# Row-tiled cluster products two at a time on the banks of the attention sums, and two filler pieces moved into the first group norm

## The chip, the cores and the metric

The kernel runs on one core of a Trainium2 chip. The metric is device time in microseconds (us), 3557.26 as the median of three runs. A core has TensorE (matrix products, written to the eight banks of PSUM), VectorE, ScalarE and GpSimd (elementwise work; GpSimd does not touch PSUM in this kernel), and queues that move data.

## What is computed

Four images of 256 channels and 64 × 64 pixels go through two layers, all in f32. Layer 0 is self-attention over the 4096 pixels with a residual:

```
attn = softmax(q k)            # 4096 x 4096 per image
x    = gamma * (v attn) + x
```

Layer 1 begins with a group norm over the whole image (`gn1`), then clusters the pixels, and adds the result to x:

```
out = sim * agg                # each pixel gets its cluster's mean, for each head
y   = x + ls1 * (proj_w out + proj_b)
```

A second group norm (`gn2`) over y, a two-layer perceptron with gelu, another residual, and a final 1 × 1 convolution with relu follow. The group norms need sums over a whole image before their first output can be had.

## The kernel before

The order of the instructions on every engine is written out by hand; each engine works its own list in that order, and an instruction waits until what it reads is there and what it overwrites is free. The main loop runs over the four images (`b`, called batches here). For each one `weighting` does the attention's sums, `cluster` the first norm and the clustering, and `mlp` the rest, including scores of the next image.

**Fillers.** While an image is in the stages with little TensorE work, TensorE is fed pieces of the next image's projections. `projections` (line 592) is a list of 35 pieces: 32 calls of `v_half` (line 271: two matmuls, and after every second call a copy by ScalarE, line 286), with `k_half(0)`, `q_four(0)` and `k_half(1)` put in ahead of number 26. `fill(n)` takes the next n pieces. Before the change they went: 8 in `weighting`, 2 in `gn1`, 10 in `cluster` ahead of the products, 4 and 9 among the products (lines 916 and 922), 2 in `gn2`. The last image has no next one, so its `fill` does nothing.

**The first norm** (`group_norm`, line 203): VectorE aggregates the statistics, TensorE averages them over the partitions (`gnm_gn`, lines 209 and 210; `gnv_gn`, line 219), `rsqrt` (line 151) goes through ScalarE and VectorE with the pooling between, and VectorE forms scale and shift. `cluster` then scales the pooled values (line 626), and TensorE makes `pcen` from them (line 631), `len` and `wc` (lines 670 to 675), and the large `fv` (line 762).

**The products.** `products(hb, c)` (line 867) adds the projected clusters to the pixels: `hb` is a half of the rows, `c` a half of the channels, and q = 0 to 3 are four matmuls of 32 rows by 512 columns, each in its own 32 rows of the array and its own PSUM bank, so that four can run at once. For c = 0 the banks are those of `ps_s` (two tiles of two banks), and VectorE adds directly (line 898). For c = 1 they were `a0` and `a1` of `ps_a`, in which the weighting sums, and both banks of `ps_m`; ScalarE scales each into a tile `cl` (line 908; three of them rotate), and GpSimd adds it (line 909). `seen` (line 863) takes the statistics of the second norm on VectorE. Those feed `bn_aggr` (line 207) and `gnm_gn` of `gn2`.

**Who else uses the banks.** `v_half`, `k_half` and `q_four` write banks of `ps_m`, which rotate in the order of allocation. `gnm_gn` and `gnv_gn` use `a0` and `a1`.

Of the kernel before, what the change touches and what calls it, by code (L numbers as in the profile page):

```python
# [8 lines left out]
F32 = mybir.dt.float32  # L9
AF = mybir.ActivationFunctionType  # L10
ALU = mybir.AluOpType
AX = mybir.AxisListType

P = 128
# [3 lines left out]
NB = 512  # L18
# [27 lines left out]
def attention_then_cluster_block(  # L46
# [17 lines left out]
    nc = tc.nc  # L64
# [9 lines left out]
    ps_a = ctx.enter_context(tc.tile_pool(name="ps_a", bufs=1, space=PSUM))  # L74
    ps_m = ctx.enter_context(tc.tile_pool(name="ps_m", bufs=2, space=PSUM))
# [67 lines left out]
    def par(name, k=None):  # L143
        i = PC.index(name)
        return pc_s[:, :, i] if k is None else pc_s[:, k, i : i + 1]
# [5 lines left out]
    def rsqrt(dst, src, eps, meanwhile=lambda: None):  # L151

        nc.vector.tensor_scalar(dst, src, eps, None, ALU.add)
        nc.scalar.activation(dst, dst, AF.Sqrt)
        meanwhile()
        nc.vector.reciprocal(dst, dst)
# [42 lines left out]
    def table(f):  # L199

        nc.scalar.activation(probe, probe, f)

    def group_norm(b, which, stats, fill, meanwhile=lambda: None):

        nm = f"{which}_{b}"
        mv = small.tile([P, 2], F32, tag="mv", name=f"mv_{nm}")
        nc.vector.bn_aggr(mv, stats.rearrange("p i s -> p (i s)"))
        ps1 = ps_a.tile([P, NB], F32, tag="a0", name=f"gnm_{nm}")
        nc.tensor.matmul(ps1[:, 0:1], left, mv[:, 0:1], start=True, stop=True)
        nc.tensor.matmul(ps1[:, 1:2], avg, mv[:, 0:1], start=True, stop=True)  # L210
        fill(1)
        dv = small.tile([P, 2], F32, tag="dv", name=f"dv_{nm}")
        nc.vector.tensor_copy(dv, ps1[:, 0:2])
        nc.vector.scalar_tensor_tensor(
            mv[:, 1:2], dv[:, 0:1], dv[:, 0:1], mv[:, 1:2], ALU.mult, ALU.add
        )
        nc.vector.tensor_scalar(dv[:, 1:2], dv[:, 1:2], -1.0, None, ALU.mult)
        ps2 = ps_a.tile([P, NB], F32, tag="a1", name=f"gnv_{nm}")
        nc.tensor.matmul(ps2[:, 0:1], avg, mv[:, 1:2], start=True, stop=True)
        rstd = small.tile([P, 1], F32, tag="rstd", name=f"rstd_{nm}")  # L220
        rsqrt(rstd, ps2[:, 0:1], GN_EPS, meanwhile)
        fill(1)
        if which == "gn2":
            table(AF.Gelu_apprx_tanh)
        ga = small.tile([P, KC], F32, tag="ga", name=f"ga_{nm}")
        gb = small.tile([P, KC], F32, tag="gb", name=f"gb_{nm}")
        nc.vector.tensor_scalar(ga, par(f"{which}_w"), rstd, None, ALU.mult)
        nc.vector.scalar_tensor_tensor(gb, ga, dv[:, 1:2], par(f"{which}_b"), ALU.mult, ALU.add)
        return ga, gb
# [369 lines left out]
    def cluster(b, ys, stats, cells, rest, fill):  # L599

        pool = small.tile([P, KC, 4, 4], F32, tag="pool", bufs=1, name=f"pool_{b}")

        def pooling():
# [3 lines left out]
            nc.vector.tensor_scalar(pool, pool, 1.0 / 256, None, ALU.mult)  # L607

        ga, gb = group_norm(b, "gn1", stats, fill, pooling)
        xns = {}  # L610

# [138 lines left out]
        for nb in range(NBLK):  # L750
# [18 lines left out]
            for g in range(2):  # L769
                q = 2 * fh + g  # L770
# [89 lines left out]
        stats2 = small.tile([P, 2 * NBLK, 6], F32, tag="stats", name=f"st2_{b}")  # L860
        pieces = {}

        def seen(hb, c):
            for q in range(4):
                nc.vector.bn_stats(stats2[:, 4 * q + 2 * hb + c, :], pieces[hb, c][q])

        def products(hb, c):
            if c == 0:
                two = [
                    ps_s.tile([P, 2, NB], F32, tag="s", name=f"op_{b}_{hb}_{c}_{f}")  # L870
                    for f in range(2)
                ]
                ops = [two[q // 2][:, q % 2, :] for q in range(4)]
            else:
                ops = [
                    pool.tile([P, NB], F32, tag=tag, name=f"op_{b}_{hb}_{c}_{q}")
                    for q, (pool, tag) in enumerate(
                        ((ps_a, "a0"), (ps_a, "a1"), (ps_m, "m"), (ps_m, "m"))
                    )
                ]  # L880
            for q in range(4):
                rows = slice(q * 32, (q + 1) * 32)
                nc.tensor.matmul(  # L883
                    ops[q],
                    g_s[rows, c * P : (c + 1) * P],
                    sim_t[rows, hb, :],
                    start=True,
                    stop=True,
                )
            pieces[hb, c] = yqs = [  # L890
                ys[2 * (q // 2) + hb][:, c, :].rearrange("p (h f w) -> p f h w", h=16, f=2)[
                    :, q % 2
                ]
                for q in range(4)
            ]
            for q in range(4):
                if c == 0:
                    nc.vector.scalar_tensor_tensor(  # L898
                        yqs[q],
                        ops[q].rearrange("p (h w) -> p h w", h=16),  # L900
                        par("ls1", c),
                        yqs[q],
                        ALU.mult,
                        ALU.add,
                    )
                else:
                    add = work.tile([P, NB], F32, tag="w", bufs=3, name=f"cl_{b}_{hb}_{q}")
                    nc.scalar.activation(add, ops[q], AF.Identity, scale=par("ls1", c))  # L908
                    nc.gpsimd.tensor_tensor(
                        yqs[q], add.rearrange("p (h w) -> p h w", h=16), yqs[q], ALU.add  # L910
                    )

        products(0, 0)
        products(0, 1)
        seen(0, 0)
        fill(4)
        products(1, 0)
        products(1, 1)
        seen(0, 1)
        seen(1, 0)  # L920
        seen(1, 1)
        fill(9)
        return stats2


    def mlp(b, ys, stats2, fill, nxt):

        ga, gb = group_norm(b, "gn2", stats2, fill)
        fill(N)
        ob = out[b].rearrange("(k p) h w -> p k (h w)", p=P)  # L930
# [97 lines left out]
    def filler(todo):  # L1028
        def fill(n):
            for _ in range(min(n, len(todo))):  # L1030
                todo.pop(0)()

        return fill

    with tc.manual_schedule():
        here = attention(0, xs0)
        here.alone()
        for b in range(B):
            xs1 = []
            nxt = attention(b + 1, xs1) if b + 1 < B else None  # L1040

            def ahead():
                if nxt and len(xs1) < N // XT:
                    xs1.append(load_x(b + 1, len(xs1)))

            fill = filler(list(nxt.projections) if nxt else [])
            stats, cells, rest = here.weighting(ahead, fill, (lambda: None) if b else derived)
            stats2 = cluster(b, here.xs, stats, cells, rest, fill)
            mlp(b, here.xs, stats2, fill, nxt)
            here = nxt  # L1050
# [76 lines left out]
```

## Time and profile before

| What | Value |
|---|---|
| median of 3 runs | 3557.26 us (3555.52 to 3558.32) |
| profiled span | 3554.6 us |
| mean granted TensorE clock | 0.990 |
| attention sums `av` (line 389) on the chain that ended last | 50% |
| products `op` (line 883), 64 matmuls | 128 records, 587 ns each |
| `cl` (line 908), 32 times | 687 ns each |

The page gives the share of the span in which each engine was busy, and the chain of work that ended last, followed back from the end. The list of waits says which instruction waited for which, in total, how often, and the longest time. The timeline has one row for neighbouring instructions of one line: start, length, engine, line, what is written and read, the number of records, and in brackets the idle time of the engine ahead and what ended it. PE is TensorE's matmul, PEld its weight load, DVE VectorE, ACT ScalarE, POOL GpSimd. PEclk is the share of its full clock that TensorE was granted.

### The profile page before, as it was taken

The page shows a single profiled execution, that of the slowest core. Times are in us where ns is not written, and L with a number is a line of the kernel's source. Part 1 is how long each engine was busy: PE and PEld are TensorE (multiplying, and loading weights), DVE is VectorE, ACT ScalarE, POOL GpSimd, SP SyncE. Part 2 cuts the span into 40 slices and gives each one's busy share as a digit, 9 for nine tenths or more (in the row PEclk, how much of TensorE's full clock was granted, in tenths as well). Part 3 has the DMA queues.
Part 4 walks back from the last instruction along what each step waited for, and adds up shares of the span by engine and source line. Part 5 has one row for each costly group of instructions (what it writes and reads, how often), then busy time and mean ns, then how long its engine had stood idle before and what let it go on. Part 6 is the DMA issues. An engine that isn't in the chain of part 4 may idle for free.

```text
span 3554.6 us, 28614 instructions
## 1 busy us (share of the span) xinstructions
PE 3467.7 (98%) x11016; PEld 1570.0 (44%) x11016; DVE 1699.8 (48%) x1972; ACT 1560.3 (44%) x1765; POOL 1380.2 (39%) x660
## 2 busy tenths in 40 slices
PE   8999999999999999999999999999999999997899
PEld 4344445644444444654444444464444444445444
DVE  3666664411366666441146666743115666664100
ACT  4555552433454554343354554533335554542222
POOL 1565665100265665410035665631004666672000
PEclk9999999999999999999999999999999999998999
DMA  2000001000000000000000000100000000000000
GB/s 89 7 4 3 6 1 48 7 18 18 12 6 4 3 6 20 29 13 12 18 15 4 3 6 3 47 1 13 18 18 9 4 6 3 4 0 1 12 18 18
DMA packets 25368, 46.93 MB, mean 13 GB/s; under 512 B 6704, under 2 KB 8592, under 8 KB 25232
## 3 DMA queue, kind: packets, MB, share of 16 engines
q1 hardware_dynamic: 20240, 38.29, 3.2%
q10 hardware_dynamic: 4992, 6.82, 0.8%
q8 instruction: 86, 1.41, 0.2%
q14 instruction: 50, 0.41, 0.0%
HBM read 19.93 MB, written 16.78 MB: 10 GB/s over the span
## 4 chain that ended last, share of the span: by engine, by line
PE 94%; DVE 3%; ACT 1%; issue 0%; DMA 0%; SPq 0%; ACTq 0%
PE av L389 50%; PE h L991 13%; PE mo L980 12%; PE sc L326 8%; PE pw L951 3%; PE vp L278 2%; PE fv L762 2%; PE mb L364 1%; PE den L410 1%; PE qp L297 0%; PE kp L255 0%; PE tt L350 0%; DVE vf L771 0%; PE op L883 0%; DVE x L898 0%
## 5 line engine op out<-in xcount | busy, mean ns | idle before, releaser
L389 PE MATMUL av<-s,v 128*128 128x512 f32 x4096 | 1826.5, 597 | 1.3 <-ACT s L379 1.3
L384 POOL TENSOR_TENSOR acc<-acc,s 128x1024 f32<-128x1024 f32 x448 | 1058.3, 2362 | 470.3 <-ACT s L379 450.7
L389 PEld LDWEIGHTS av<-s,v 128*128 128x128 f32 x4096 | 758.9, 190 | 1025.3 <-issue 1015.8
L379 ACT ACTIVATE s<-s 128x1024 f32<-128x1024 f32 x512 | 539.0, 1057 | 464.6 <-DVE s L376 431.4
L336 DVE TENSOR_TENSOR top<-sc,top 128x1024 f32<-128x1024 f32 x224 | 274.2, 1224 | 714.5 <-PE sc L326 714.5
L376 DVE TENSOR_TENSOR s<-s,mb 128x1024 f32<-128x1024 f32 x512 | 595.0, 1206 | 8.6 <-PE mb L364 8.3
L381 POOL TENSOR_TENSOR acc<-s 128x1024 f32<-128x1024 f32 x32 | 75.2, 2349 | 1133.9 <-ACT s L379 1133.9
L991 PE MATMUL h<-xn,w_s 128*128 128x512 f32 x1024 | 480.9, 597 | 4.6 <-DVE xn L937 4.6
L980 PE MATMUL mo<-hs,w_s 128*128 128x512 f32 x1024 | 476.0, 592 | 0.0
L332 ACT COPY s<-sc 128x1024 f32<-128x1024 f32 x256 | 258.5, 1010 | 406.4 <-PE sc L326 406.4
L999 ACT ACTIVATE hs<-h,pv_s 128x512 f32<-128x512 f32 x256 | 176.1, 688 | 478.6 <-PE h L991 478.6
L991 PEld LDWEIGHTS h<-xn,w_s 128*128 128x128 f32 x1024 | 192.8, 191 | 255.4 <-issue 249.6
L980 PEld LDWEIGHTS mo<-hs,w_s 128*128 128x128 f32 x1024 | 194.6, 190 | 244.9 <-issue 239.2
L337 ACT COPY s<-sc 128x1024 f32<-128x1024 f32 x256 | 259.3, 1013 | 91.6 <-DVE top L336 50.3
L339 DVE TENSOR_TENSOR top<-sc,top 128x1024 f32<-128x1024 f32 x224 | 274.4, 1225 | 49.7 <-ACT s L332 30.0
L326 PE MATMUL sc<-q,k 32*128 32x512 f32 x2048 | 295.1, 640 | 2.7 <-ACT s L337 2.7
L1018 DVE SCALAR_TENSOR_TENSOR x<-mo,pc_s,x 128x512 f32<-128x512 f32 x64 | 48.1, 751 | 495.9 <-PE mo L980 492.5
L326 PEld LDWEIGHTS sc<-q,k 32*128 32x128 f32 x2048 | 81.9, 182 | 194.8 <-issue 109.1
L278 PE MATMUL vp<-wv_s,x 128*128 128x256 f32 x512 | 132.4, 407 | 21.1 <-ACT cl L908 11.7
L278 PEld LDWEIGHTS vp<-wv_s,x 128*128 128x128 f32 x512 | 98.0, 200 | 49.6 <-ACT cl L908 16.6
L951 PE MATMUL pw<-xn,wpw_s 128*128 128x512 f32 x256 | 115.5, 594 | 0.8 <-ACT xn L1021 0.8
L334 DVE TENSOR_TENSOR top<-sc,s 128x1024 f32<-128x1024 f32 x32 | 39.2, 1225 | 146.4 <-ACT s L332 146.4
(166 smaller groups left out, 1652.6 us busy)
## 6 DMA issues: line engine op xcount, KB each, us to landing
x<-in_x SPq DMA_DIRECT2D x32, 512.0 KB, 4.7
out<-xn SPq DMA_DIRECT2D x64, 256.0 KB, 2.1
q<-q ACTq DMA_DIRECT2D x104, 64.0 KB, 2.0
w_s<-in_w SPq DMA_DIRECT2D x2, 1024.0 KB, 7.6
q<-q SPq DMA_DIRECT2D x24, 64.0 KB, 2.0
wv_s<-in_wv SPq DMA_DIRECT2D x1, 256.0 KB, 6.9
wpw_s<-in_wpw SPq DMA_DIRECT2D x1, 256.0 KB, 9.5
wfv_l<-in_wfv SPq DMA_DIRECT2D x1, 192.0 KB, 3.0
```

What stands on the lines that cost most here:

```text
L278: nc.tensor.matmul(vps[0][:, i % 2, :], xs[i * P // XT][:, k, o : o + P], wv_s[:, k, :], start=(k == 0), stop=(k == KC - 1),)
L326: nc.tensor.matmul(halves[r // 2][:, r % 2, :], k_s[rows, g, :], q_s[rows, :], start=True, stop=True)
L332: nc.scalar.copy(s[:, 0:2, :], halves[0])
L336: nc.vector.tensor_tensor(top, halves[1], top, ALU.max)
L337: nc.scalar.copy(s[:, 2:4, :], halves[1])
L339: nc.vector.tensor_tensor(top, halves[0], top, ALU.max)
L376: nc.vector.tensor_tensor(sh, sh, mxs[nb].unsqueeze(1).to_broadcast([P, 2, NB]), ALU.subtract)
L379: nc.scalar.activation(sh, sh, AF.Exp)
L384: nc.gpsimd.tensor_tensor(acc, acc, s[:, 2 * h : 2 * h + 2], ALU.add)
L389: nc.tensor.matmul(av[c], own["v"][:, RG * g + quarter, c * P : (c + 1) * P], slots[u][:, quarter, :], start=(g == 0 and quarter == 0), st ...
L980: nc.tensor.matmul(acc[c], w2_s[:, j, c * P : (c + 1) * P], hs[j], start=(j == 0), stop=(j == HID // P - 1),)
L991: nc.tensor.matmul(ps, w1_s[:, k, j * P : (j + 1) * P], xn[:, 0, k, :], start=(k == 0), stop=(k == KC - 1),)
```

## The change

The second channel half of the products (c = 1) now goes two at a time, q = 0 and 1 and then q = 2 and 3, both on `a0` and `a1`; `ps_m` is left to the fillers. Between the two pairs stand two filler pieces. The fillers are spread anew: two more in the first norm (where `fill(1)` becomes `fill(3)`), then 2, 2, 2 and 5 among the products. That is for keeping TensorE supplied while ScalarE empties the banks. In the third of these places the pieces are `k_half(0)` and `q_four(0)`. Which numbers are computed does not change.

```diff
-        fill(1)
+        fill(3 if which == "gn1" else 1)
...
-        def products(hb, c):
+        def products(hb, c, qs):
...
-                ops = [two[q // 2][:, q % 2, :] for q in range(4)]
+                ops = {q: two[q // 2][:, q % 2, :] for q in qs}
             else:
-                ops = [
-                    pool.tile([P, NB], F32, tag=tag, name=f"op_{b}_{hb}_{c}_{q}")
-                    for q, (pool, tag) in enumerate(
-                        ((ps_a, "a0"), (ps_a, "a1"), (ps_m, "m"), (ps_m, "m"))
-                    )
-                ]
-            for q in range(4):
+                ops = {
+                    q: ps_a.tile([P, NB], F32, tag=f"a{q % 2}", name=f"op_{b}_{hb}_{c}_{q}")
+                    for q in qs
+                }
+            for q in qs:
...
-        products(0, 0)
-        products(0, 1)
+        products(0, 0, range(4))
+        products(0, 1, (0, 1))
         seen(0, 0)
-        fill(4)
-        products(1, 0)
-        products(1, 1)
+        fill(2)
+        products(0, 1, (2, 3))
+        fill(2)
+        products(1, 0, range(4))
+        products(1, 1, (0, 1))
+        fill(2)
+        products(1, 1, (2, 3))
         seen(0, 1)
         seen(1, 0)
         seen(1, 1)
-        fill(9)
+        fill(5)
```

More of the change, by code (lines that the diff above doesn't have):

```diff
@@ L864, in seen @@
             for q in range(4):
-                nc.vector.bn_stats(stats2[:, 4 * q + 2 * hb + c, :], pieces[hb, c][q])
-        def products(hb, c):
+                nc.vector.bn_stats(stats2[:, 4 * q + 2 * hb + c, :], pieces[hb, c, q])
+        def products(hb, c, qs):
             if c == 0:
@@ L889, in products @@
                 )
[L890 to L896, printed above, removed]
+            for q in qs:
+                y = pieces[hb, c, q] = ys[2 * (q // 2) + hb][:, c, :].rearrange(
+                    "p (h f w) -> p f h w", h=16, f=2
+                )[:, q % 2]
                 if c == 0:
                     nc.vector.scalar_tensor_tensor(
-                        yqs[q],
+                        y,
                         ops[q].rearrange("p (h w) -> p h w", h=16),
                         par("ls1", c),
-                        yqs[q],
+                        y,
                         ALU.mult,
@@ L909, in products @@
                     nc.gpsimd.tensor_tensor(
-                        yqs[q], add.rearrange("p (h w) -> p h w", h=16), yqs[q], ALU.add
+                        y, add.rearrange("p (h w) -> p h w", h=16), y, ALU.add
                     )
-        products(0, 0)
-        products(0, 1)
+        products(0, 0, range(4))
+        products(0, 1, (0, 1))
         seen(0, 0)
-        fill(4)
-        products(1, 0)
-        products(1, 1)
+        fill(2)
[5 more added lines that the diff above has]
+        products(1, 1, (2, 3))
         seen(0, 1)
```

## The prediction

> **What bounds the kernel now.** I read the page first, its engine line and its chain that ended last:
>
> ```profile
> PE 3467.7 (98%) x11016; PEld 1570.0 (44%) x11016; DVE 1699.8 (48%) x1972; ACT 1560.3 (44%) x1765; POOL 1380.2 (39%) x660
> ...
> PE 94%; DVE 3%; ACT 1%; issue 0%; DMA 0%; SPq 0%; ACTq 0%
> ```
>
> TensorE is the bound nearly everywhere. So a change pays where it takes TensorE's idle time away, or where it raises the granted clock. Next, the list of TensorE's waits (total us, times, longest); two of its lines lie in the edited stages:
>
> ```profile
> PE gnm_gn L209 <- DVE mv_gn L207: 17.0, 5, 10.8
> PE vp L278 <- ACT cl L908: 11.7, 6, 2.0
> ...
> PE pcen L631 <- DVE pool L626: 8.4, 4, 2.8
> ```
>
> The second line is six waits of a filler (`v_half`) on the scaling copy `cl`, two in each of batches 0 to 2: the filler wants a bank of `ps_m` that products 2 and 3 of the second half still occupy. The third is the gap in the first norm, ahead of the pooled centres. Batch 0's timeline shows both in place (columns: start, length, instruction, and in brackets the idle time ahead):
>
> ```profile
> 613.20 1.11 PE L278 MATMUL vp<-wv_s,x 128*128 128x256 f32 x4
> 616.17 0.48 PE L631 MATMUL pcen<-pool,mix 128*96 128x16 f32 x4 [1.85 <-DVE pool L626]
> ...
> 621.25 5.07 PE L762 MATMUL fv<-mix,xn 128*128 128x208 f32 x20
> ```
>
> ```profile
> 661.81 2.00 PE L883 MATMUL op<-simt,g 32*128 32x512 f32 x16
> 665.72 3.72 PE L278 MATMUL vp<-wv_s,x 128*128 128x256 f32 x16 [1.91 <-ACT cl L908]
> 669.37 2.00 PE L883 MATMUL op<-simt,g 32*128 32x512 f32 x16
> 673.35 1.99 PE L278 MATMUL vp<-wv_s,x 128*128 128x256 f32 x8 [1.98 <-ACT cl L908]
> ```
>
> Each f32 matmul leaves two records here, so a `v_half` is four records and two sets of four products are sixteen. The bracketed waits show 3.89 us of idle TensorE per batch around the products, and 1.85 us in the norm. Last, the busy time and granted clock of successive windows behind that norm (columns: window; length; busy time of PE, PEld, DVE, ACT, POOL with instruction counts; PEclk; DMA):
>
> ```profile
> 613.83:617.24 3.41, 1.56 (x11) 1.10 (x9) 2.73 (x11) 1.40 (x2) 0.00 (x0) 1.00 0.00 0
> 617.24:620.65 3.41, 3.41 (x13) 2.80 (x12) 2.46 (x9) 0.96 (x2) 0.00 (x0) 0.50 0.02 5
> 620.65:624.06 3.41, 3.41 (x11) 3.15 (x11) 0.00 (x0) 0.59 (x1) 0.00 (x0) 0.50 0.00 0
> 624.06:627.47 3.41, 3.41 (x21) 3.41 (x20) 1.22 (x4) 1.52 (x2) 0.56 (x1) 1.00 0.00 0
> ```
>
> After a stretch with only 1.56 us of work in 3.41, TensorE runs at half clock for 6.8 us. The same happens from 1487.6 (busy 1.55) and from 2361.4 (busy 1.55). Around the products only one gap did it: 1542.25 to 1545.67 was busy for 1.45 us, and 3.41 us at half clock followed. Windows there with 1.92 us of work or more stayed at full clock.
>
> [...] sixteen records in 2.00 us is two sets of four, some 0.86 us a set once the 0.15 us tail is taken off. [...] The trace's cost is small: from 665.72 to 669.37 is 3.65 us for 16 filler records, which at their pace elsewhere (24 in 5.25 us, 0.219 each) need 3.50, hence 0.15 going in; coming back out of a tiled mode (678.74 to 680.58) takes 0.12 more than the preceding 1.72 us step.
>
> **The change, part by part.**
>
> Two fillers into the first norm: two `v_half`, 2 × 4 × 0.219 = 1.75 us. The run of three begins at 613.20 and ends about 615.9; `pcen` started at 616.17, because VectorE's pooled values came at 616.03. So they lie inside the wait, at no cost, and 1.75 us of filler leave the product stage. ScalarE gets one copy more (0.59 us) there, which pushes the first norm's activation from 615.73 to about 616.6; its output is not needed before `fv` starts, so nothing is paid.
>
> The clock behind it: with the gap filled, the window has over 3 us of work, and the clock should stay. At full clock `vp` behind `pcen` ends near 617.4, `len` starts at 617.6 (VectorE's operand is ready at 617.55), the `wc` group ends about 618.8, the next `vp` 0.88 us later, and `fv` starts at 619.8 in place of 621.25. That is 1.45 us; the cold 2.8 us of `fv` up to 624.06 shrink by half, 1.4 us. Batch 0 gains 2.85. In the other batches `pcen` to `fv` takes 5.89 and 5.12 us where 3.65 will do, and `fv` was cold for 0.9 and 2.4 us: 2.24 + 0.45 and 1.47 + 1.2. Together **8.2 us**; the other end is 0, if the clock drops anyway.
>
> The products: counted from their start (661.81), the next norm's `gnm` stands at 22.3 us (684.14). Removed: 3.89 us of waits, 1.75 us of filler. Added: two products no longer run beside two others, so the second half costs two sets of 0.86 instead of one, twice a batch: 1.72. There are also two more trips from full array to row tiles and back, 2 × 0.27, and two returns that the old wait hid, 2 × 0.12: 0.8 (bounds 0.3 and 2). Sum −3.1 us.
>
> New waits: products 2 and 3 need the banks `a0`, `a1` that `cl` of products 0 and 1 frees. Those copies start 2.0 us after the products and take 0.69 us each at a pace of 0.62, so the banks are free at 3.3; two fillers keep TensorE to 3.6. The wait is hidden. Behind the second group stand `k_half` and `q_four`, 1.7 us each, so hidden as well. `ps_s` for the next `products` call is freed by VectorE at 3.9 and needed at 6.8.
>
> VectorE could take over: its last statistics need GpSimd's last addition, now behind the last pair. Pair at 12.3 to 13.2, `cl` to 14.7, GpSimd (1.24 us each) to 16.6; the statistics, 0.615 us each and in order, end at 18.1 and the aggregate at 18.7, against 19.2 before. So `gnm` can start at about 18.9 on VectorE's account and 19.2 on TensorE's. Take **3.1 us** for batches 0 and 2; batch 1 also loses its half-clock window (`vp` 2.88 against 1.99, `kp` 2.67 against 1.93): 1.6 more with the rest, 4.7. Sum 10.9.
>
> Batch 3 has no fillers. There VectorE is busy without a break from 3279.66 to 3295.13 with the same instructions; the pair waits for `cl`, but that engine has its work anyway. I charge 0.2 us (0 to 0.8). The new places of the remaining fillers change no total.
>
> **Sum**: 8.2 + 10.9 − 0.2 = 18.9, from 3557.26: **3538.4 us**, 0.53% less.
>
> **The rivals.**
> A. The clock drops in the first norm all the same: `len` and `wc` stream only 64 columns, and may not count as activity. For it: in batch 0 the first cold window had records end to end and did not bring the clock back. Against: with two more fillers the full-array work alone is over half of each window. Gain 10.9 − 0.2: 3546.6.
> B. The second pair's wait takes the place of the one removed, if the bank is released later than the copy's end. Then 3.89 us stay, 2.5 are added and 1.75 leave: each product stage costs 0.8 more, and only the first norm gains: 3557.3 − 8.2 + 2.4 + 0.2 = 3551.7. Against: by the times above the copies are ahead of the fillers by 0.3 us.
> C. Slower: both of these, and the broken-up tiles, with bubbles in each mode change (2 us a batch), let the clock drop once per product stage (3.41 us at half, 1.7 lost). 3557.3 + 3 × (0.8 + 1.2 + 1.7) + 0.8 = 3569.2. Against: 1.92 us in a window kept the clock.
> D. VectorE's chain reaches the second norm 2 us later than I have it, because `k_half` and `q_four` sit ahead of the last pair: product gains fall to 1.3, 3 and 1.3 us: 3543.7.
>
> **How the numbers follow.** Forecast 0.64, A 0.13, D 0.10, B 0.08, C 0.05. The time is the forecast's. [...] each remaining gap may or may not drop the clock: about 1.7 us each, some 3 us over a run. The low end is the forecast less 5 (smaller mode-change cost, no drop at all), 3533. The high end takes in A and D: 3549. Faster by over 0.2% is below 3550.1: the forecast, A and D and a third of B, with something off for what I can't see, 0.88; within 0.2%, 0.07; slower, 0.05.
>
> **What would show it.** In the profile after: the wait of `vp` on `cl` gone from the list, and none of `op` on `cl` in batches 0 to 2 above some tenths; `pcen`'s wait down from 8.4 us to about 3 (batch 3's own 2.8 stays); PEclk 1.00 from 613 to 627; `gnm` 19 us after the products' start. Wrong it would be if half clock still stands behind the norm, if `op` waits for `cl`, or if `gnm` waits for VectorE by over 1 us in batches 0 to 2.

## The result, and the profile after

The changed kernel takes 3539.06 us (median of 4 runs, 3536.81 to 3543.42) where the kernel before takes 3557.79 beside it: a ratio of 0.995, 95% interval 0.9933 to 0.9967. Measured again later, it was 3541.69 against 3556.71, 0.9957 (0.9945 to 0.997). The nine runs of both measurements part by their mean granted clock: four between 3536.8 and 3539.4 us at 0.992, five between 3541.4 and 3543.4 at 0.991. The profiled spans are 3537.6 and 3554.6 us, a difference of 17.0.

TensorE's waits in the changed kernel (total us, times, longest):

```profile
...
PE vp L278 <- ACT v L286: 10.8, 5, 4.9
...
PE pcen L631 <- DVE pool L626: 2.8, 1, 2.8
...
PE op L881 <- ACT cl L903: 1.0, 2, 0.8
```

The wait of `vp` on `cl` is gone. `pcen` waits once, in batch 3, which has no fillers. The two new waits of the products on `cl` are batch 3's as well. What is left of `vp` on the copy `v` is partly at the very start of the program, and three times 1.86 us in the clustering; it comes up again below.

The timeline of the first norm of batch 0, with the three fillers in one run, and then that of the products:

```profile
614.30 2.84 PE L278 MATMUL vp<-wv_s,x 128*128 128x256 f32 x12
617.27 0.48 PE L631 MATMUL pcen<-pool,mix 128*96 128x16 f32 x4
...
620.73 22.77 PE L762 MATMUL fv<-mix,xn 128*128 128x208 f32 x128
...
660.02 1.99 PE L881 MATMUL op<-simt,g 32*128 32x512 f32 x12
661.93 1.99 PE L278 MATMUL vp<-wv_s,x 128*128 128x256 f32 x8
663.86 1.13 PE L881 MATMUL op<-simt,g 32*128 32x512 f32 x4
664.91 1.99 PE L278 MATMUL vp<-wv_s,x 128*128 128x256 f32 x8
666.84 1.99 PE L881 MATMUL op<-simt,g 32*128 32x512 f32 x12
668.75 1.93 PE L255 MATMUL kp<-x,wqk_s 128*32 128x256 f32 x32
670.50 1.90 PE L297 MATMUL qp<-x,wqk_s 128*32 128x512 f32 x16
672.34 1.13 PE L881 MATMUL op<-simt,g 32*128 32x512 f32 x4
673.39 1.93 PE L255 MATMUL kp<-x,wqk_s 128*32 128x256 f32 x32
675.26 3.72 PE L278 MATMUL vp<-wv_s,x 128*128 128x256 f32 x16
678.81 0.28 PE L209 MATMUL gnm_gn<-mv_gn,left 128*128 128x1 f32 x2
```

No row among the products carries a bracket: TensorE waits for nothing between 660 and 679. Twelve records are four products and a pair, in the time that two sets of four took (1.99 us, and 2.00 for the sixteen records before the change). A pair alone takes 1.05 us from its start to the next row's. And `pcen` follows the fillers with no wait.

The granted clock behind the first norm (window; length; busy time of PE, PEld, DVE, ACT, POOL; PEclk; DMA) stays at 1.00 where it was 0.50 for 6.8 us:

```profile
614.00:617.00 3.00, 3.00 (x16) 2.45 (x14) 2.35 (x8) 0.79 (x2) 0.00 (x0) 1.00 0.00 0
617.00:620.00 3.00, 2.78 (x19) 2.22 (x19) 2.01 (x9) 1.79 (x4) 0.00 (x0) 1.00 0.00 0
620.00:623.00 3.00, 3.00 (x17) 2.64 (x16) 1.29 (x5) 1.05 (x2) 0.00 (x0) 1.00 0.00 0
```

Where the 17.0 us come from is seen by taking the starts of the same instructions from both timelines, batch by batch (us between starts):

| Stretch | before, batches 0, 1, 2, 3 | after, batches 0, 1, 2, 3 | gain in 0 to 2 |
|---|---|---|---|
| `gnm` (gn1) to `pcen` | 4.52, 4.52, 4.52, 4.94 | 4.52, 4.52, 4.52, 4.93 | 0.0 |
| `pcen` to `fv` | 5.08, 5.89, 5.12, 4.10 | 3.46, 3.46, 3.46, 4.10 | 5.7 |
| `fv` to products | 40.56, 39.62, 40.42, 42.55 | 39.29, 39.55, 39.28, 44.45 | 2.5 |
| products to `gnm` (gn2) | 22.33, 23.96, 22.33, 16.80 | 18.79, 18.79, 18.80, 16.80 | 12.2 |

The edited stages of batches 0 to 2 gain 20.4 us. Three stretches that the change does not touch give some back in this pair of profiles: `fv` to the products in batch 3 (+1.9), the start up to the first `gnm` (+1.1), and the tail behind batch 3's `h` (+0.5). Batch 3's share is mostly clock: in the changed kernel's profile TensorE stood at half clock for the first 5.5 us of its `fv`, before the change for 2.7, and for longer behind `cnt`.

### The profile page after: what moved, and what is told of

Same layout as the page of the kernel before. It is cut to its first block, busy times and chain, and to the rows that moved or that the text cites. A ratio compares the mean times of both kernels' runs of the same rounds, so it can differ in the third digit from the quotient of the medians.

```text
span 3537.6 us, 28598 instructions
## 1 busy us (share of the span) xinstructions
PE 3468.3 (98%) x11016; PEld 1564.1 (44%) x11016; DVE 1699.9 (48%) x1972; ACT 1560.0 (44%) x1765; POOL 1380.7 (39%) x660
## 4 chain that ended last, share of the span: by engine, by line
PE 95%; DVE 3%; ACT 1%; DMA 0%; issue 0%; SPq 0%; ACTq 0%
PE av L389 50%; PE h L990 13%; PE mo L979 12%; PE sc L326 8%; PE pw L950 3%; PE fv L762 2%; PE vp L278 2%; PE mb L364 1%; PE den L410 1%; PE op L881 1%; PE qp L297 0%; PE kp L255 0%; PE tt L350 0%; DVE vf L771 0%; DVE st L865 0%
```

## The experiments

All were timed in turn with the kernel before, on the same chip; each time is a median with the one of the kernel before beside it.

**One half of the change at a time.** First the fillers alone:

```diff
-        fill(1)
+        fill(3 if which == "gn1" else 1)
...
-        fill(9)
+        fill(7)
```

> The two fillers in the first norm alone, products as before. Theory (two separate gains, gap and clock): pcen starts when it did (4.5 us after gnm), fv 3.5 us after pcen at full clock, so 8.2 us over batches 0 to 2; 1.75 us of filler leave each product stage, which still waits 1.9 us twice for cl. 3557.8 - 8.2 - 5.3 = 3544.3. Rival (the gain is the freed banks, and the norm gives nothing): 3552 or more.

Measured: 3545.5 against 3556.75, ratio 0.9968 (0.9956 to 0.9979). `pcen` to `fv` is 3.46 us in all three batches, as in the changed kernel, and `gnm` to `pcen` is still 4.52: the two fillers cost nothing where they stand. The product stage takes 22.09, 22.09 and 20.40 us; in batch 1 its sixteen filler records ran 5.41 us for 3.72 behind the wait for `cl` of 1.92 us: 1.7 more, as much as 3.41 us at half clock cost, so the wait seems to have taken the clock with it there. The six runs part by the clock too: three from 3541.3 to 3542.4 us at a mean of 0.992, three from 3548.6 to 3549.7 at 0.990. The profile is of one of the latter, and shows a half-clock stretch in batch 1 between `cnt` and the products:

```profile
1518.00:1520.00 2.00, 0.37 (x2) 0.00 (x0) 1.64 (x5) 1.97 (x4) 0.00 (x0) 1.00 0.00 0
1520.00:1522.00 2.00, 1.77 (x10) 1.60 (x10) 1.19 (x3) 0.66 (x2) 0.00 (x0) 0.78 0.00 0
1522.00:1524.00 2.00, 2.00 (x17) 1.88 (x20) 0.01 (x1) 0.00 (x0) 0.00 (x0) 0.50 0.00 0
```

The stretch from `cnt` to the products took 8.62 us there and 5.57 in the other batches. It follows the wait of `vp` on the copy `v`, the gap of 1.86 us in the clustering.

Then the pairs alone:

```diff
-        fill(3 if which == "gn1" else 1)
+        fill(1)
...
-        fill(5)
+        fill(7)
         return stats2
```

> The pairs on a0 and a1 alone, one filler in the first norm as before; the third place among the products gets two v_half, the rest goes to the end. Theory: the waits for cl are gone, the first norm keeps its 1.85 us gap and its 6.8 us at half clock. From the trace after, the product stage gains 3.5, 5.2 and 3.5 us, less the 1.75 us of filler that stays in it: 7 us over three batches, 3551. With the first run this adds up to the whole change (13.5 + 7). Rival (the pairs cost more than the waits did): 3558 or more.

Measured: 3549.52 against 3556.75, 0.9978 (0.997 to 0.9986). The product stage takes 20.59, 20.58 and 20.58 us; `pcen` to `fv` 5.07, 4.75 and 5.34, so the half clock is there. The two halves give 11.3 and 7.2 us, 18.5 together; the whole change gave 18.7, and 15.0 when measured again. That the sum is so close is partly luck, since the first median lies between its two groups of runs. The stages are the firmer test: each half shows its own gain in its own stage, and not the other's.

**Gap or clock.** To see the clock without moving any filler, spare matmuls that nobody reads went into the gap of the kernel before:

```diff
         fill(1)
+        if which == "gn1" and b + 1 < B:
+            busy = ps_m.tile([P, NB], F32, tag="m", name=f"busy_{b}")
+            for i in range(4):
+                nc.tensor.matmul(
+                    busy[:, (i % 2) * C : (i % 2) * C + C], ident, w2_s[:, i, :], start=True, stop=True
+                )
```

> The kernel before, plus four spare full-array f32 matmuls of 256 columns (1.75 us, their output is read by nobody) in the first norm of batches 0 to 2 where the two fillers would go. No filler is moved. Theory: only the clock gains, 8.2 us: 3549.6, PEclk 1.00 behind pcen, fv 3.5 us after pcen. Rival (the gain in the norm is the filler work taken away elsewhere, the clock is no cause): 3557.8 or more.

Measured: 3550.92 against 3556.75, 0.9986 (0.9979 to 0.9992), so 5.8 us from work that computes nothing. Batch 0, with the spare matmuls in the gap:

```profile
614.84 1.89 PE L226 MATMUL busy<-w_s,ident 128*128 128x256 f32 x8
616.86 0.48 PE L637 MATMUL pcen<-pool,mix 128*96 128x16 f32 x4
```

`pcen` to `fv` is 3.46 and `fv` to `cnt` 33.70 in all three batches, as in batches 0 and 2 of the changed kernel: in these two stretches of the profile the whole gain is there, 8.5 us. Of it, the profile lost some in the product stage, which took 23.95 us in two batches in place of one, the half-clock value.

The same place with matmuls of one column:

```diff
+            for i in range(8):
+                nc.tensor.matmul(
+                    busy[:, i : i + 1], (ident, avg)[i % 2], ones[:, 0:1], start=True, stop=True
+                )
```

> As the run before, but eight spare matmuls of one column (128 x 128 weights, about 0.22 us each with their two weight loads, so 1.8 us of TensorE time with almost nothing streamed). If the clock follows the time in which TensorE has any instruction: 3549.6, as with full matmuls. If it follows streamed columns, the clock drops behind pcen as before: 3557.8. I lean to the second, 0.65.

Measured: 3556.23 against 3556.75, 0.9998 (0.999 to 1.0006): nothing. The gap ahead of `pcen` is filled but for 0.18 us, and still the clock drops in batches 0 and 2: the four filler records behind `pcen` take 1.61 and 2.05 us there, and 1.11 in batch 1, which kept it. Timeline and windows of batch 0:

```profile
615.04 0.36 PE L226 MATMUL busy<-ones,avg 128*128 128x1 f32 x2
615.58 0.48 PE L637 MATMUL pcen<-pool,mix 128*96 128x16 f32 x4 [0.18 <-DVE pool L632]
```

```profile
612.00:616.00 4.00, 3.82 (x30) 3.58 (x30) 2.85 (x11) 1.60 (x3) 0.00 (x0) 1.00 0.02 4
616.00:617.00 1.00, 1.00 (x5) 0.71 (x4) 0.83 (x5) 0.00 (x0) 0.00 (x0) 0.69 0.00 0
617.00:618.00 1.00, 1.00 (x6) 0.92 (x5) 0.55 (x2) 0.00 (x0) 0.00 (x0) 0.50 0.00 0
```

PE was busy for 3.82 of 4 us and lost half its clock behind it. So the busy column did not tell here whether the clock holds. Streamed columns are what the full spare matmuls have in the same 1.8 us and these lack: 5.8 us gained with the ones, 0.5 with the others.

The profiles of the kernel before and of the changed one allow a closer look. In both, the time between two changes of the clock is 3.41 us or a whole multiple of it, from 3.41 to 3174.4. On the grid of 3.41 us that these changes lie on, the busy time of TensorE in a window does not part those ahead of a drop from the others: before the change the drops of batches 0 to 2 came behind windows busy for 1.45 to 1.57 us; in the changed kernel the window from 1515.43 us was busy for 1.55 and kept the clock, and the one from 3266.47 was busy for 2.85 and lost it.

An estimate of the work on the array parts them better. It is made from the records of these two profiles: 0.43 us for a record of 512 columns that uses all 128 × 128 of the array (the `av` records at full clock start 0.43 us apart), and less in proportion to columns and to the part of the array used. Of the 2,030 windows at full clock in the two profiles, the 14 that half clock followed held an estimated 1.18 us or less, the others 1.27 or more. Of the 37 at half clock, the 12 that full clock followed held 1.31 us or more, the others 1.21 or less. The estimate moves by 0.1 to 0.2 us with the place in a record to which the work is put, so it gives no exact limit. In the one-column run, the window from 612.97 us was busy for 3.23 us and held an estimated 1.03 of work. This is a fit to two profiles; the experiment behind it is the pair of spare runs.

**What hides the wait for the banks.** Both pairs at once, fillers behind:

```diff
-        fill(2)
         products(0, 1, (2, 3))
-        fill(2)
+        fill(4)
         products(1, 0, range(4))
         products(1, 1, (0, 1))
-        fill(2)
         products(1, 1, (2, 3))
+        fill(2)
```

> The changed kernel with the second pair of each half right behind the first, and the two fillers behind it. Theory (the fillers hide the wait for the banks): cl of products 0 and 1 ends 3.3 us after the start, TensorE is there at 1.9, so op waits about 1.3 us for cl twice in each of batches 0 to 2; 0.27 us of mode change are saved each time. Six times 1.0: 3545. Rival (the banks are free early enough, the fillers between are needless): 3537.

Measured: 3548.42 against 3556.58, 0.9977 (0.9969 to 0.9985), 7 to 9 us slower than the two medians of the changed kernel. In batch 0, the second pair of the first half and the fillers behind it:

```profile
661.55 1.70 PE L881 MATMUL op<-simt,g 32*128 32x512 f32 x4 [0.77 <-ACT cl L903]
663.17 3.72 PE L278 MATMUL vp<-wv_s,x 128*128 128x256 f32 x16
```

The wait is 0.77 us ahead of the pair, and the pair takes 1.62 in place of 1.05 because its second product waits for its own bank: 1.3 together, as expected. The rest is clock again: the product stage took 23.04, 23.03 and 21.35 us, and in the first `k` and `q` ran at a slower pace (3.08 and 2.50 us against 1.93 and 1.90). Half clock came there behind a window that was busy for 2.58 of 3.41 us, but in part with a lone pair, which uses two times 32 of the array's 128 rows (an estimated 1.10 us of work, at the same 0.43 us a full record).

**How close VectorE is.** Two more fillers ahead of the last pair:

```diff
         products(1, 1, (0, 1))
-        fill(2)
+        fill(4)
         products(1, 1, (2, 3))
...
-        fill(5)
+        fill(3)
         return stats2
```

> The changed kernel with two more fillers ahead of the last pair (k_half, q_four, k_half, v_half) and three behind in place of five. Theory (VectorE's chain through the last pair, ScalarE, GpSimd and the statistics is level with TensorE's list): gnm waits for mv_gn by about 2.3 us in each of batches 0 to 2, 3539 + 7 = 3546. Rival (VectorE has room to spare): within 1 us of 3539.

Measured: 3549.72 against 3556.58, 0.998 (0.9972 to 0.9988). The product stage takes 21.08 us in all three batches, 2.3 more:

```profile
680.75 0.35 PE L209 MATMUL gnm_gn<-mv_gn,left 128*128 128x1 f32 x2 [2.06 <-DVE mv_gn L207]
```

In size the step is as expected, 6.9 us (3 × 2.3) of the 8 to 11 that the time grew; batch 1's profile has another half-clock stretch ahead of the products (8.44 us from `cnt`), and in batches 0 and 1 half clock also followed the new wait: the last four filler records behind it take 1.70 and 1.85 us, for 1.11 at full clock. So the two engines were level in the changed kernel, and the last pair can't move back.

**Two tries at the remaining gap** in the clustering. First, more fillers ahead of `summed`, one fewer behind `similar(1)`:

```diff
-        fill(2)
+        fill(4)
         summed(lambda j, q: pool_w[:, j], True)
...
-        fill(5)
+        fill(4)
         largest(1)
...
-        fill(5)
+        fill(4)
         return stats2
```

> The changed kernel with fillers spread otherwise in the clustering: four ahead of summed (two before) and four behind similar(1) (five before), the one in all taken from the five behind the last pair. The wait of vp for the copy v, 1.86 us in each of batches 0 to 2, stands behind ScalarE's tanh and table loads; with two pairs copied ahead of them it should go. One filler more is absorbed (0.9 us) and cnt starts 0.3 us earlier: 3 x 1.2 = 3.6 us, 3535.4. Rival (VectorE's ranking ends last there, the wait only changes its name): 3538 to 3540.

Measured: 3545.88 against 3556.58, 0.9971 (0.9961 to 0.9982): 4 to 7 us slower than the two medians of the changed kernel. A miss. In the changed kernel the copy `v` at 652.86 us, batch 0, does stand behind two table loads of ScalarE, 1.28 us each. But here the wait only has a new name and about the same length:

```profile
650.66 1.57 PE L811 MATMUL cnt<-scr,ones 128*96 128x64 f32 x16 [2.04 <-DVE scr L732]
```

`fv` to `cnt` did fall to 33.37 us, by the 0.3 expected. But `cnt` and the second half of `agg`, which stream few columns, now follow 2 us of idle time directly, and the clock was halved in all three batches (7.1 to 7.3 us from `cnt` to the products, against 5.6; in batch 0 PEclk is 0.50 from 654 to 656 us). And because the list is shifted by one piece, the second place among the products holds `v_half` and `k_half`: longer, so VectorE came late by 0.8 us (19.61 to `gnm`).

The second try keeps the order, and gives pieces 20 and 21 a bank that does not hang on ScalarE's list:

```diff
             if i % 2 == 0:
-                vps[0] = ps_m.tile([P, 2, C], F32, tag="m", name=f"vp_{b}_{i // 2}")
+                if b and i == 20:
+                    vps[0] = ps_s.tile([P, 2, 2, C], F32, tag="s", name=f"vp_{b}_{i // 2}")[:, 0]
+                else:
+                    vps[0] = ps_m.tile([P, 2, C], F32, tag="m", name=f"vp_{b}_{i // 2}")
...
-        fill(5)
+        fill(6)
         largest(1)
...
         products(0, 1, (2, 3))
-        fill(2)
+        fill(1)
```

> The changed kernel again, beside the two runs that follow, on the same chip. 3539, within 3 us.

> The changed kernel, in which v pieces 20 and 21 go to a bank of ps_s, which is idle behind fv, and six fillers stand behind similar(1) in place of five; the second place among the products gets one in place of two. Theory (the earlier redistribution failed because the pieces only moved ahead of VectorE's ranking, and because a longer second place made VectorE late): no wait of vp for the copy v in batches 0 to 2, fv to cnt 33.4 us, the idle stretch ahead of cnt under 0.9 us, so no half clock there; products to gnm 17.9 us in place of 18.8. 3 x 1.25 = 3.8 us under the changed kernel, 3535. Rival (VectorE's chain ends last at the second norm): products to gnm stays at 18.8, 3538 to 3539.

Measured: 3533.56 for the second try, 3541.69 for the changed kernel beside it, 3556.71 before; 0.9933 (0.9921 to 0.9946). Batch 0:

```profile
647.82 5.45 PE L281 MATMUL vp<-wv_s,x 128*128 128x256 f32 x24
654.03 1.57 PE L814 MATMUL cnt<-scr,ones 128*96 128x64 f32 x16 [0.76 <-DVE scr L735]
```

Six fillers run without a break, 0.76 us of idle time is left, and `cnt` to the products is 5.65 us in all three batches, while the changed kernel beside it shows 5.57, 6.54 and 6.80. Products to `gnm` falls to 17.9. The stages account for 3.4 us of the 8.1: `gnm` to `h` takes 68.4 to 68.7 us, where undisturbed batches of the changed kernel take 69.5 to 69.8. The clock in the clustering is the likely rest: in the profile of the changed kernel beside it, half clock there cost 3.3 us in batches 1 and 2 together, and the mean granted clock was 0.991 in four of its five runs, against 0.993 in four of five here. One profile each can't show where it dropped in the other runs.

**The batch without fillers.** Batch 3 got 35 spare pieces of two full-array matmuls, in the places where the others have fillers:

```diff
-            fill = filler(list(nxt.projections) if nxt else [])
+            def spare():
+                busy = ps_m.tile([P, NB], F32, tag="m", name=f"busy_{b}_{len(spares)}")
+                for i in range(2):
+                    nc.tensor.matmul(
+                        busy[:, :C], ident, w2_s[:, i, :], start=True, stop=True
+                    )
+                spares.append(busy)
+
+            spares = []
+            fill = filler(list(nxt.projections) if nxt else [spare] * 35)
```

> The changed kernel with 35 spare full-array pieces for batch 3, each as long as a v_half (output read by nobody), in the places where the other batches have fillers. Theory (the clock is a gain of its own): gnm to h in batch 3 takes 69.5 us as in the others in place of 74.3, h starts at full clock: 5 to 6 us less, 3533.5. Rival (batch 3 is bound by VectorE, the clock does not matter there, and spare work may get in the way): 3539 to 3541.

Measured: 3534.87 against 3556.58, 0.994 (0.9928 to 0.9953). `gnm` to `h` in batch 3 takes 70.2 us in place of 74.2, though the spare pieces lengthen its product stage (18.6 us for 16.8), and what follows `h` takes 253.2 in place of 255.8. Its mean granted clock is 0.997, where the changed kernel's was 0.992. With the second try on top:

> The run before and the spare pieces of batch 3 together: 3.8 and 4.2 us add up, 3531. If they share a cause, 3534.

Measured: 3527.98 against 3556.71, 0.9918 (0.9904 to 0.9932). This is the fastest version, about 14 us under the changed kernel beside it; 5.6 of that come from spare work.

## Why the prediction was right

The forecast was 3538.4 us; 3539.06 was measured, and 3541.69 in the repeat. The mechanism came as forecast, but to hit within 0.7 us was partly luck: the products gave 1.3 us more than forecast, stretches that the change does not touch took 3.5 back in that pair of profiles, and the nine runs spread over 6.6 us with the clock. Step by step:

- **Two fillers in the gap of the first norm, free.** Right: `gnm` to `pcen` is 4.52 us before and after, with and without them.
- **The clock behind it, 8.2 us.** Right in cause, and in size as the profiles show it: 5.7 + 2.5 us. The run with spare full matmuls shows it without any filler moved, though its time fell by only 5.8. The drop came after windows busy for 1.45 to 1.57 us of 3.41, and in the one-column run after a stretch with hardly any idle time (3.82 of 4 us busy). The estimated work on the array fits both, idle time does not. So the prediction's 1.92 us of busy time, with which windows of the kernel before stayed at full clock, is no safe mark: in other runs half clock followed windows busy for 1.98 us (more fillers ahead of `summed`) and 2.58 us (both pairs at once).
- **The products, 10.9 us.** Right in kind, measured 12.2. The term that was mis-sized is the mode changes: the split was charged 2.52 us per batch (1.72 for the sets, 0.8 for mode changes). Measured, it is 18.79 − (22.33 − 3.89 − 1.75) = 2.10, so the mode changes cost 0.38 net. In this trace each way costs about 0.2 us: eight filler records ahead of a pair take 1.93 us where 1.75 would do, and the pair 1.05 where its streaming takes an estimated 0.86 (two records of 512 columns at 0.43, with the two products side by side). The net is smaller, and a likely reason is that the old order paid such changes too: ahead of `k_half` the eight records of `v_half` took 1.92 us before the change, and that step is gone. The bounds of 0.3 and 2 us in the forecast, and the 2 us of rival C, were the author's estimates. A pair and a set of four stream equally long: a set and a pair took 1.99 us, two sets 2.00; and a record of these 32-row products took 587 ns in the mean before the change, one of `av` with 128 rows and as many columns 597.
- **The banks are free when the second pair comes.** Right: no wait in batches 0 to 2. Without the fillers between, 1.3 us of waiting come back at each pair.
- **VectorE at 18.9, TensorE at 19.2.** Nearly: the aggregate ends 18.5 us after the products' start and `gnm` stands at 18.8. The late-pair run shows that 2.9 us of further pieces ahead of the last pair push `gnm` back by 2.3.
- **Batch 3, 0.2 us.** It cost nothing: 16.80 us from the products to `gnm` in both.
- **Rival A** was wrong for fillers, but part of its premise was seen: the eight one-column matmuls did not keep the clock in two batches of three. **Rival B** needs the fillers away, and then its wait is there. C and D did not come.

What the sum did not hold is the gap of 1.86 us in the clustering. I had allowed about 3 us in a run for half-clock windows there and elsewhere, at 1.7 us each, an estimate; a hit costs 1 to 3 us in one batch. That such a gap may or may not drop the clock is seen in the fillers-only run: `cnt` to the products took 8.62 us in one batch and 5.57 in two. In the changed kernel's two profiles it came in two batches of six, and the second try's gain beyond its 3.4 us suggests that it comes often. The exact rate per run was not measured.

## What to carry to other kernels

A gap of under 2 us on the bounding engine can cost more than its own length: here 1.85 us of idle time took another 2 to 3 us with it, through the clock. So look at PEclk in the windows behind each gap before pricing it, and fill it with matmuls that stream many columns over the whole array: here four of 256 columns, with nothing else moved, gained 5.8 us, and eight of one column 0.5. When a filler waits for a bank, ask on which engine's list the bank's release is queued: another bank, free for another reason, made the move of one filler pay, where a new order alone did not.

## What the runs showed of the hardware

- One-column matmuls with full weight loads, 0.22 us apart, did not hold TensorE's clock in two batches of three, with PE shown as busy for 3.82 of 4 us.
- In the profiles before and after, changes of the clock lay 3.41 us or a whole multiple of it apart. The 14 full-clock windows of 3.41 us that half clock followed held an estimated 1.18 us of work on the array or less, the 2,016 others 1.27 or more. The estimate is good to 0.1 or 0.2 us, so no exact limit follows.
- Half-clock stretches in batches 0 to 2 of the profile before were 3.41 or 6.83 us long; in batch 3 without fillers, before and after, 10.24 to 17.07. Whether the gap of 1.86 us in the clustering brought one changed from batch to batch and run to run. The fillers-only runs fell in two groups, 3541.3 to 3542.4 us at a mean clock of 0.992 and 3548.6 to 3549.7 at 0.990; the profile is of the second, and has such a stretch in batch 1.
- Work whose output nobody reads made the program faster, by 5.8 us in the first norms and 5.6 us in the last batch.
